# Two-layer cross-attention on one core: image scores copied by VectorE, and the second pair's two norm products side by side

## The chip, the core and the metric

The kernel runs on one core of a Trainium2 chip. A core has a matrix engine (TensorE, called PE in the profile, with its weight loads shown apart as PEld), VectorE (DVE), ScalarE (ACT), GpSimd (POOL) and SyncE (SP, which here only issues transfers). Each engine works through its own queue in order; they wait for each other by semaphores. Matmuls write to PSUM, a small memory of eight banks per partition; VectorE and ScalarE read their results from there. The metric is the device time of one execution in microseconds.

## The reference

Two cross-attention layers with image prompts follow each other, on 16 batches of 256 query positions and 320 channels, 20 heads of 16. The context has 256 rows of 512 features. The first layer takes 77 rows as text and the other 179 as image tokens; the second takes 252 as text and the last 4 as image tokens. The part that matters here is the second layer, cut to its core:

```python
q, k_t, v_t = heads(hidden @ W_q), heads(text @ W_k), heads(text @ W_v)
probs_t = softmax(q @ k_t.T * 0.25)
text_out = probs_t @ v_t
attn = q @ heads(ip @ W_k_ip).T * 0.25            # 4 image scores per query and head
qsem = l2norm(probs_t @ text)                     # per head, 512 features
sem = qsem @ l2norm(ip).T
probs_ip = softmax(attn + 0.5 * sem) * spatial_mask
out = (text_out + probs_ip @ v_ip) @ W_out + b_out + hidden
```

The length of `probs_t @ text` is needed for `l2norm`. The kernel gets its square as p^T G p, where G = text text^T is one matrix for each batch: it multiplies G with the probabilities, multiplies the product element by element with the probabilities, and sums over the text rows. These are the "norm products" below.

## The kernel before, in words

Work goes in *slots*: one slot is one batch and one group of four heads, so there are 5 slots for a batch, 80 (`NS`) for the first layer and 80 for the second, one after the other. What PE does, and in which order, is written out by hand in `slot0` and `slot1`: a slot yields functions, which are run at that place, and numbers such as 0.33, 0.67 and 1.0. At a number, `fill(k + number)` runs all tasks that are due by then (projections, keys, values, closing of a batch), each with a table of due times. So a number in `slot1` is a place for other work. On PE this program order is also the order on the chip. For VectorE, ScalarE, POOL and SP the order is planned when the kernel is built, from dependencies and estimated times; `queued` adds an order-only edge that puts an instruction behind the last `anchor` of its engine.

In the second layer, slot k does the following on PE.

- `attend1(k - 2)` (lines 855 to 864) makes the weighted values of the slot two before: sixteen matmul records in line 861, and then the *zone* matmuls of line 863 with their eight records. These add the column sums of `W[k, u][:, 0]`, the finished squared lengths, for the two head pairs u = 0 and 1. They need the sums of line 853.
- `both1(k, 0)` and, later, `both1(k, 1)` (lines 773 to 800) do the transposed scores of slot k (tile T, line 787), and the plain scores of slot k + 2 (tile S, line 792, two banks and one buffer). VectorE takes the maxima over the text columns of S (line 793), ScalarE the exponentials of T (line 798) into P, and `image_scores` copies the four image columns of each head out of S (line 810, 128 x 16 elements).
- `norm1(k - 1, u, n)` (lines 843 to 853) is a norm product for pair u, half n: four matmuls of 512 columns for n = 0, three for n = 1 (line 848), into a bank of the tag X. VectorE multiplies the result with W (line 851); for u = 1 and n = 1 it writes the result back to the PSUM bank, and VectorE then adds it to the first half in line 853. For u = 0 POOL does that addition.
- `rounded1(k, u)` (lines 834 to 839) prepares the next slot's products: ScalarE rounds half of P (line 838, tile ctb), POOL takes the difference to P (line 839, tile wt). The rounded halves go to two buffers in turn, so the rounding of pair u waits until the previous slot's products of that pair have read theirs.
- `maxima(k + 2)` (lines 822 to 832) turns the maxima by two small matmuls (line 826), ScalarE copies them (line 828) and issues two transfers that write them to the query rows.
- `stacks(k + LEAD)` loads the rows of queries and keys for a later slot by SP.

The other matmuls of that layer come from fills: line 212 (keys, values and G of the next batch), line 519 (projections of queries and outputs; their results are read out by lines 527 and 528, or 766), line 969 (closing of a batch, read by lines 970, 747, 749 and 751). All of these and the norm products use the tag X, with three buffers.

Of the kernel before, what the change touches and what calls it, by code (L numbers as in the profile page):

```python
# [10 lines left out]
AF = mybir.ActivationFunctionType  # L11
# [17 lines left out]
SCALE = 0.25  # L29
# [8 lines left out]
NS = B * NG  # L38
# [10 lines left out]
def xattn2(  # L49
# [27 lines left out]
    nc = tc.nc  # L77
# [11 lines left out]
    def bank(tag="X"):  # L89
        return ps.tile([128, 512], F32, tag=tag, name=tag, bufs=BANKS[tag])  # L90

    def scores():

        return ps.tile([128, 1024], F32, tag="S", name="S", bufs=1).rearrange("p (h t) -> p h t", h=4)
# [4 lines left out]
    def buf(tag, shape, dtype=F32, bufs=1, name=None):  # L99
        if tag in ("wB", "wD", "vr", "raw"):  # L100
            return sb.tile(shape, dtype, tag=tag, name=name or tag, bufs=bufs)
        size = 1
        for d in shape[1:]:
            size *= d
        if tag not in slots:
            slots[tag] = [0, dtype] + [const_tile([128, max(size, words.get(tag, 0))], f"{tag}_{i}", dtype) for i in range(bufs)]
        n, kind, *ring = slots[tag]
        assert kind == dtype and len(ring) == bufs, tag
        slots[tag][0] += 1
        t = ring[n % bufs][: shape[0], :size]  # L110
        names = "abcd"[: len(shape) - 1]
        if len(names) > 1:
            t = t.rearrange(f"p ({' '.join(names)}) -> p {' '.join(names)}", **dict(zip(names, shape[1:])))
        return t
# [17 lines left out]
    def queued(inst, *behind):  # L132

        for other in behind or [anchors.get(inst.ins.engine)]:
            if other is not None:
                tc.add_manual_dep(
                    inst.ins, other.ins.name, mybir.DependencyInfo(mybir.DependencyClass.NoSync, mybir.DependencyReason.DATA), reason="order"
                )
        return inst

    def anchor(inst):
        anchors[inst.ins.engine] = inst
        return inst
# [459 lines left out]
    QK, P, W, R = {}, {}, {}, {}  # L603
# [76 lines left out]
    def attend0(k):  # L680
        b, g = divmod(k, NG)
        v, pv = get("v0", b), bank("P")
        for vt in range(3):
            values0(k, pv, v, vt)
        settle0(b, g, pv)
# [87 lines left out]
    def both1(k, t):  # L773

        a = k + 2 < 2 * NS and QK[k + 2] 
        c = NS <= k < 2 * NS and QK[k]
        if a:
            if t == 0:
                maxes[k + 2] = buf("mn", [128, 4, 4], FR, bufs=2)[:, :2]
            sp = scores()  # L780
        if c:
            st = [bank("T").rearrange("p (h t) -> p h t", h=2) for u in range(2)]
            lo = (0, DUP)[t]
            for j in range(2):
                for u in range(2):
                    rows = slice(64 * u, 64 * u + KS1)
                    mm(st[u][:, j], c[1][rows, j, lo : lo + 128], c[0][rows, j], start=True, stop=True)  # L787
        if a:
            for j in range(2):
                for u in range(2):  # L790
                    rows = slice(64 * u, 64 * u + XROW)
                    mm(sp[:, 2 * u + j], a[0][rows, j, t * 128 : (t + 1) * 128], a[1][rows, j], start=True, stop=True)  # L792
            anchor(nc.vector.tensor_reduce(maxes[k + 2][:, t], sp[:, :, :T1], axis=AX.X, op=ALU.max))  # L793
        if c:
            for u in range(2):
                if t == 0:
                    P[k, u] = buf("P", [128, 2, 2, S], bufs=SIZES["NP"])
                anchor(queued(nc.scalar.activation(P[k, u][:, t], st[u], AF.Exp, scale=SCALE)))  # L798
        if a:
            image_scores(k + 2 - NS, t, sp)  # L800

    sims = {}

    def image_scores(n, t, sp):
        b, g = divmod(n, NG)
        if (g, t) == (0, 0):
            sims[b] = buf("sr", [128, 2, 4, NG, NIP], bufs=2)
        sr = sims[b]
        src = sp.rearrange("p (u j) t -> p u j t", u=2)[:, :, :, T1:]
        anchor(nc.scalar.copy(sr[:, t, :, g].rearrange("p (j u) n -> p u j n", u=2), src))  # L810
        if (g, t) == (NG - 1, 1):
            later(0.3, lambda: image_scores_out(b))

    def image_scores_out(b):
        sid = dram.tile([S, 4, NG * NIP], F32, tag="sid", name="sid", bufs=2)
        dma(sid.rearrange("(t p) s c -> p t (s c)", p=128), sims[b].rearrange("p t s g n -> p t (s g n)"))
        si = results["si", b] = buf("si", [128, 8, NG * NIP], bufs=2)
        parts = sid.rearrange("(f r) s c -> r s f c", r=32)
        for s in range(4):
            later(1.3, lambda s=s: dma(si[32 * s : 32 * s + 32], parts[:, s]))  # L820
# [13 lines left out]
    def rounded1(k, u):  # L834
        R[k, u] = buf("ctb", [128, 2, 2, S], FR, bufs=SIZES["CTB"], name="ph")
        W[k, u] = buf("wB", [128, 2, 2, S], bufs=SIZES["WB"], name="wt")
        for t in range(2):
            nc.scalar.activation(R[k, u][:, t], P[k, u][:, t], AF.Copy, scale=0.5)  # L838
            anchor(nc.gpsimd.tensor_sub(W[k, u][:, t], P[k, u][:, t], f(R[k, u][:, t])))  # L839
# [3 lines left out]
    def norm1(k, u, n):  # L843

        gm = get("t1", k // NG - B)[1]
        yp = bank().rearrange("p (h t) -> p h t", h=2)
        for i, (gb, kt) in enumerate(blocks[n]):
            mm(yp, gm[:, gb], R[k, u][:, kt], start=i == 0, stop=i == len(blocks[n]) - 1)  # L848
        w = W[k, u]
        product = yp if n and u else w[:, n]  # L850
        nc.vector.tensor_mul(product, yp, w[:, n])  # L851
        if n:
            (nc.vector if u else nc.gpsimd).tensor_add(w[:, 0], w[:, 0], product)  # L853

    def attend1(k):
        b, g = divmod(k - NS, NG)
        v, pv = get("t1", b)[0], bank("P")
        for n in range(2):
            for s in range(4):
                h = V1W * (4 * g + s)  # L860
                mm(pv[32 * s : 32 * s + 32, :S], v[:, n, h : h + 32], P[k, s % 2][:, n, s // 2], start=n == 0, stop=False)  # L861
        for s in range(4):
            mm(pv[32 * s : 32 * s + 32, :S], zone, W[k, s % 2][:, 0, s // 2], start=False, stop=True)  # L863
        settle1(b, g, pv)

    def slot1(k):
        last = k - 1 if NS < k <= 2 * NS else None
        mine = k < 2 * NS
        if k == NS:
            yield lambda: maxima(k + 1)  # L870
        elif k == NS + 1:
            yield lambda: attend0(k - 2)
        else:
            yield lambda: attend1(k - 2)
        yield lambda: both1(k, 0)
        if last:
            yield lambda: norm1(last, 0, 0)
        yield 0.33
        if last:
            yield lambda: norm1(last, 0, 1)  # L880
        yield lambda: both1(k, 1)
        if mine:
            yield lambda: rounded1(k, 0)
        yield lambda: stacks(k + LEAD)
        if last:
            yield lambda: norm1(last, 1, 0)
        yield 0.67
        if last:
            yield lambda: norm1(last, 1, 1)
        if mine:  # L890
            yield lambda: rounded1(k, 1)
        yield lambda: maxima(k + 2)
        yield 1.0

# [124 lines left out]
    def later(slots, make):  # L1019
        delayed.append((clock[0] + slots, make))  # L1020
# [26 lines left out]
    for c in range(B // 2):  # L1047
        n, k = 10 * c, [("k0", c)] if c else []
# [11 lines left out]
    for b in range(B):  # L1060
        n = NS + 5 * b
# [17 lines left out]
    def stacks(k, parts="KQ"):  # L1079
        if 0 <= k < NS:  # L1080
            stacks0(k, parts)
        elif k < 2 * NS and "K" in parts:
            stacks1(k)

    def ahead(k, t):
        if k < NS:
            score0(k, t)
        else:
            both1(k - 2, t)

    def maxima(k):
        if k < 2 * NS:
            (maxima0 if k < NS else maxima1)(k)
# [43 lines left out]
    with tc.manual_schedule(engines=PINNED):  # L1137
        for k in range(2 * NS + 2):
            clock[0] = k
            for part in (slot0 if k < NS else slot1)(k):  # L1140
                if callable(part):
                    part()
                else:
                    fill(k + part)
        fill(999)
# [81 lines left out]
```

## Time and profile before

| | us |
|---|---|
| median of 3 runs | 1545.48 (1541.51 to 1552.83) |
| the profiled execution | 1544.94 |
| its span, first to last instruction | 1542.8 |
| PE busy | 1475.5 (96%) |
| VectorE busy | 1166.4 (76%) |
| ScalarE busy | 967.6 (63%) |
| POOL busy | 1146.1 (74%) |

The mean granted clock of PE is 0.987 of full speed. Busy means that at least one instruction of the engine was under way. Matmuls are pipelined and their ends are modelled, so PE's share overstates how well it is used: a wait of some tenths of a microsecond can lie inside a "busy" stretch. Start times of groups tell more than their lengths. A row of the timeline gives start, length, engine, line, operation, tiles and count; a bracket gives the idle time before it and what ended it. A row of the waits gives the waiting engine, tile and line, what it waited for, total us, times, and the longest. A row of groups ends with busy us, mean ns of one, and the idle time before.

### The profile page before, as it was taken

How to read it: one execution, taken by the hardware profiler on the slowest of the kernel's cores; microseconds unless marked ns; L12 is line 12 of the kernel's file. 1: busy time of each engine (PE TensorE's matmuls, PEld its weight loads, DVE VectorE, ACT ScalarE, POOL GpSimd, SP SyncE). 2: the span in 40 equal slices, each digit the busy share in tenths (PEclk: the TensorE clock that was granted, in tenths of full speed). 3: DMA queues.
4: the chain of work that ended last, by engine and by line, in shares of the span. 5: the costliest groups of instructions: out<-in, count | busy, mean ns of one | idle time of the engine just before them, and what ended most of it. 6: DMA issues, size and time to landing. Idle time of an engine off the chain costs nothing.

```text
span 1542.8 us, 35099 instructions
## 1 busy us (share of the span) xinstructions
PE 1475.5 (96%) x12522; PEld 1186.1 (77%) x12522; DVE 1166.4 (76%) x2424; ACT 967.6 (63%) x2233; POOL 1146.1 (74%) x1161
## 2 busy tenths in 40 slices
PE   7899999999999998899999999999999999999997
PEld 6778888888888886677777777777777777777765
DVE  5567676767677778777888778778877887888796
ACT  5567676767676866656556556655565556566563
POOL 3259797979797867886777777777787787777685
PEclk9899999999999999999999999999999999999999
DMA  7656665657565665464534443434344434433311
GB/s 218 168 166 174 168 174 161 185 149 193 149 184 150 183 172 148 117 193 133 155 98 115 130 142 94 137 112 150 90 140 124 137 99 133 134 98 112 109 30 59
DMA packets 226986, 215.38 MB, mean 140 GB/s; under 512 B 49722, under 2 KB 210716, under 8 KB 226812
## 3 DMA queue, kind: packets, MB, share of 16 engines
q1 hardware_dynamic: 225072, 211.84, 47.9%
q8 instruction: 99, 1.62, 0.5%
q10 hardware_dynamic: 1740, 1.30, 0.3%
q14 instruction: 75, 0.61, 0.1%
HBM read 122.17 MB, written 89.49 MB: 137 GB/s over the span
## 4 chain that ended last, share of the span: by engine, by line
PE 84%; DVE 7%; DMA 3%; issue 2%; POOL 1%; ACT 1%; SPq 0%; DVEq 0%; POOLq 0%; ACTq 0%
PE X L212 22%; PE X L848 18%; PE X L519 11%; PE P L710 7%; PE S L649 5%; PE T L787 4%; PE T L672 4%; PE P L861 4%; PE P L863 3%; PE S L792 3%; PE X L969 1%; PE X L568 1%; DVE X L851 1%; DVE wt L853 1%; POOL P L678 1%
## 5 line engine op out<-in xcount | busy, mean ns | idle before, releaser
L678 POOL TENSOR_TENSOR P<-P,rs 128x512 f32<-128x512 f32 x320 | 411.9, 1309 | 157.7 <-ACT P L675 157.5
L839 POOL TENSOR_TENSOR wt<-P,ctb 128x512 f32<-128x512 f32 x320 | 413.3, 1304 | 113.0 <-ACT ctb L838 108.0
L848 PE MATMUL X<-ctb,gm 128*128 128x512 f32 x1120 | 330.1, 412 | 0.8 <-DVE wt L851 0.8
L675 ACT ACTIVATE P<-T 128x512 f32<-128x512 f32 x320 | 174.9, 593 | 105.5 <-PE T L672 95.8
L798 ACT ACTIVATE P<-T 128x512 f32<-128x512 f32 x320 | 174.1, 598 | 91.2 <-PE T L787 81.6
L848 PEld LDWEIGHTS X<-ctb,gm 128*128 128x128 f32 x1120 | 189.4, 188 | 46.6 <-DVE wt L851 1.2
L838 ACT ACTIVATE ctb<-P 128x512 fp32r<-128x512 f32 x320 | 195.4, 632 | 42.5 <-PE X L848 42.3
L793 DVE TENSOR_REDUCE mn<-S 128x4 fp32r<-128x1008 f32 x160 | 191.9, 1200 | 0.5 <-PE S L792 0.5
L851 DVE TENSOR_TENSOR wt<-X,wt 128x512 f32<-128x512 f32 x240 | 163.6, 682 | 24.8 <-PE X L848 23.9
L651 DVE TENSOR_REDUCE mn<-S 128x4 fp32r<-128x716 f32 x160 | 142.4, 890 | 0.0
L710 PE MATMUL P<-P,vr 128*32 128x256 f32 x1920 | 125.0, 391 | 4.4 <-DVE mx L574 2.6
L649 PE MATMUL S<-ks,qs 125*128 125x256 f32 x640 | 116.7, 306 | 0.9 <-DVE mn L651 0.9
L649 PEld LDWEIGHTS S<-ks,qs 125*128 125x128 f32 x640 | 88.0, 193 | 34.2 <-issue 32.1
L519 PE MATMUL X<-hq,wE 128*128 128x256 f32 x768 | 109.3, 286 | 4.4 <-ACT hq L508 3.6
L519 PE MATMUL X<-ho,wF 128*128 128x256 f32 x768 | 109.0, 284 | 2.3 <-DVE ho L751 2.0
L519 PEld LDWEIGHTS X<-hq,wE 128*128 128x128 f32 x768 | 102.1, 193 | 8.1 <-ACT hq L508 4.0
L672 PE MATMUL T<-qs,ks 127*128 127x256 f32 x640 | 105.5, 288 | 1.9 <-DVE kst L148 1.9
L212 PE MATMUL X<-cta,wA 128*128 128x252 f32 (+1 forms) x720 | 100.1, 285 | 6.3 <-ACT wA L147 6.3
L853 POOL TENSOR_TENSOR wt<-wt 128x512 f32<-128x512 f32 x80 | 103.8, 1298 | 2.5 <-DVE wt L851 1.4
L519 PEld LDWEIGHTS X<-ho,wF 128*128 128x128 f32 x768 | 100.5, 190 | 6.7 <-DVE ho L751 2.7
L212 PEld LDWEIGHTS X<-cta,wA 128*128 128x128 f32 x720 | 93.1, 193 | 9.0 <-ACT wA L147 6.5
L721 DVE STREAM_TRANSPOSE nt<-P 128x512 f32<-128x512 f32 x80 | 57.0, 713 | 50.6 <-PE P L710 50.6
(199 smaller groups left out, 2948.5 us busy)
## 6 DMA issues: line engine op xcount, KB each, us to landing
qd<-q SPq DMA_DIRECT2D x96, 384.0 KB
kd<-kst SPq DMA_DIRECT2D x73, 256.0 KB
rawc<-in_cT_dram SPq DMA_DIRECT2D x60, 256.0 KB
qs<-qd SPq DMA_DIRECT2D x80, 192.0 KB
ks<-kd SPq DMA_DIRECT2D x80, 192.0 KB
ks<-kd SPq DMA_DIRECT2D x160, 96.0 KB
qs<-qd SPq DMA_DIRECT2D x160, 96.0 KB
kd<-kst SPq DMA_DIRECT2D x21, 512.0 KB
```

The lines of the kernel that those rows point to most:

```text
L212: last = mm(out, lhs(a, k), rhs(b, k), start=i == 0, stop=i == len(terms) - 1)
L519: mm(pp, w(s, k, slice(m * 128, (m + 1) * 128)), a[:, t], start=i == 0, stop=i == len(terms) - 1)
L649: mm(sp[:, h], Q[: XROW + T0, h, t * 128 : (t + 1) * 128], K[: XROW + T0, h], start=True, stop=True)
L675: exp = anchor(nc.scalar.activation(pt, st[p], AF.Exp, scale=SCALE))
L678: anchor(nc.gpsimd.tensor_mul(pt, pt, rs[:, t : t + 1].to_broadcast([128, 2, S])))
L710: mm(pv[32 * s : 32 * s + 32, o : o + S], v[:, vt, h : h + 32], P[k, s // 2][:, t, s % 2], start=vt < 2, stop=vt != 1,)
L793: anchor(nc.vector.tensor_reduce(maxes[k + 2][:, t], sp[:, :, :T1], axis=AX.X, op=ALU.max))
L798: anchor(queued(nc.scalar.activation(P[k, u][:, t], st[u], AF.Exp, scale=SCALE)))
L838: nc.scalar.activation(R[k, u][:, t], P[k, u][:, t], AF.Copy, scale=0.5)
L839: anchor(nc.gpsimd.tensor_sub(W[k, u][:, t], P[k, u][:, t], f(R[k, u][:, t])))
L848: mm(yp, gm[:, gb], R[k, u][:, kt], start=i == 0, stop=i == len(blocks[n]) - 1)
L851: nc.vector.tensor_mul(product, yp, w[:, n])
```

## The change

Two things are changed.

First, the copy of the image scores moves from ScalarE to VectorE. It is issued directly behind the maximum that reads the same score tile, is ordered behind it by `queued`, and becomes VectorE's new anchor. The exponentials become plain anchors of ScalarE: they are no longer ordered behind the last anchor there, which was the previous copy.

Second, the order inside `slot1`: the second pair's second product, `norm1(last, 1, 1)`, comes directly behind its first, `norm1(last, 1, 0)`, and `rounded1(k, 1)` behind it. The 0.67 fill, which stood between the two products, now comes after all of these. `maxima(k + 2)` stays behind the fill.

```diff
             anchor(nc.vector.tensor_reduce(maxes[k + 2][:, t], sp[:, :, :T1], axis=AX.X, op=ALU.max))
+            image_scores(k + 2 - NS, t, sp)
         if c:
             for u in range(2):
                 if t == 0:
                     P[k, u] = buf("P", [128, 2, 2, S], bufs=SIZES["NP"])
-                anchor(queued(nc.scalar.activation(P[k, u][:, t], st[u], AF.Exp, scale=SCALE)))
-        if a:
-            image_scores(k + 2 - NS, t, sp)
+                anchor(nc.scalar.activation(P[k, u][:, t], st[u], AF.Exp, scale=SCALE))
...
-        anchor(nc.scalar.copy(sr[:, t, :, g].rearrange("p (j u) n -> p u j n", u=2), src))
+        anchor(queued(nc.vector.tensor_copy(sr[:, t, :, g].rearrange("p (j u) n -> p u j n", u=2), src)))
...
         yield lambda: stacks(k + LEAD)
         if last:
             yield lambda: norm1(last, 1, 0)
-        yield 0.67
-        if last:
             yield lambda: norm1(last, 1, 1)
         if mine:
             yield lambda: rounded1(k, 1)
+        yield 0.67
         yield lambda: maxima(k + 2)
         yield 1.0
```

## The prediction

> **What bounds the kernel now.** The page comes first: the matrix engine (PE) is said to be busy 96% of the span, VectorE (DVE) 76%, ScalarE (ACT) 63%, GpSimd (POOL) 74%. Only the second layer runs the changed lines, so the next view is the table of stretches (PE, its weight loads, DVE, ACT, POOL, each with its busy time), cut where that layer's pattern repeats: 52.8 us for one batch of five slots. The first row below is the page's, the second the table's.
>
> ```profile
> PE 1475.5 (96%) x12522; PEld 1186.1 (77%) x12522; DVE 1166.4 (76%) x2424; ACT 967.6 (63%) x2233; POOL 1146.1 (74%) x1161
> ...
> 1086.80:1139.60 52.80, 52.02 (x420) 39.62 (x419) 42.31 (x81) 31.62 (x79) 39.53 (x44) 1.00 0.42 123
> ```
>
> PE 52.02 of 52.80 us looks like an engine with nothing left to win. It is not, since the ends of pipelined matmuls are modelled and a short wait is counted as busy. So I read the waits between 770 and 1500 us (total, times, longest), and then PE's own timeline.
>
> ```profile
> PE P L863 <- DVE wt L853: 10.3, 14, 0.8
> ...
> PEld P L863 <- DVE wt L853: 28.7, 44, 1.3
> ...
> ACT sr L810 <- DVE mn L793: 70.2, 81, 2.0
> ```
>
> One wait dominates on PE: the zone matmuls of line 863, for the last VectorE add of line 853. 730 us hold 13.8 batches, and 44 waits are 3.2 in each: about three slots of five. The third row is ScalarE idling until a maximum is done so that it can copy the image scores; ScalarE is the least busy engine and PE does not wait for it, so this row is worth nothing by itself. The same batch on PE (start, length, engine, line, tile, count), cut to the slots that I call A, B, C, D and E in order of time (A's zones begin at 1090.57, B's at 1101.30, C's at 1113.37, D's at 1122.25):
>
> ```profile
> 1086.33 1.19 PE L848 MATMUL X<-ctb,gm 128*128 128x512 f32 x4
> ...
> 1088.77 0.86 PE L848 MATMUL X<-ctb,gm 128*128 128x512 f32 x3
> ...
> 1090.57 0.59 PE L863 MATMUL P<-wt,zone 128*32 128x256 f32 x2
> 1091.91 0.63 PE L863 MATMUL P<-wt,zone 128*32 128x256 f32 x6 [0.75 <-DVE wt L853]
> 1092.47 0.51 PE L787 MATMUL T<-qs,ks 50*128 50x256 f32 x4
> ...
> 1097.55 1.20 PE L848 MATMUL X<-ctb,gm 128*128 128x512 f32 x4
> 1098.59 0.59 PE L969 MATMUL X<-rs,rs 128*128 128x256 f32 x2
> 1098.83 1.05 PE L848 MATMUL X<-ctb,gm 128*128 128x512 f32 x3
> 1099.71 0.28 PE L826 MATMUL X<-ident_r,mn 128*4 128x128 f32 x2
> 1099.84 0.64 PE L969 MATMUL X<-rs,rs 128*128 128x256 f32 x2
> ...
> 1101.30 0.97 PE L863 MATMUL P<-wt,zone 128*32 128x256 f32 x8
> 1102.20 0.51 PE L787 MATMUL T<-qs,ks 50*128 50x256 f32 x4
> ...
> 1110.00 1.16 PE L519 MATMUL X<-ho,wF 128*128 128x256 f32 x8
> ...
> 1113.37 0.61 PE L863 MATMUL P<-wt,zone 128*32 128x256 f32 x8
> 1113.91 0.50 PE L787 MATMUL T<-qs,ks 50*128 50x256 f32 x4
> ...
> 1118.47 1.19 PE L848 MATMUL X<-ctb,gm 128*128 128x512 f32 x4
> ...
> 1122.25 1.26 PE L863 MATMUL P<-wt,zone 128*32 128x256 f32 x8
> 1123.44 0.51 PE L787 MATMUL T<-qs,ks 50*128 50x256 f32 x4
> ...
> 1131.16 1.95 PE L212 MATMUL X<-wC,cta 128*128 128x320 f32 x12
> ```
>
> Eight zone matmuls that wait for nothing take 0.61 us (1113.37, slot C); by the start of the next group, some 0.54. Slot A needs 1092.47 - 1090.57 = 1.90, slot B 0.90, slot D 1.19. The excess is 1.36 + 0.36 + 0.65 = **2.37 us per batch**, 4.5% of it, three times the 0.78 that the busy column admits. This is the layer's removable time; the rest of PE stands back to back.
>
> **The change, part by part: the adjacent products.** PE does the same matmuls; only the second pair's second product (line 848 x3) trades places with the work of the 0.67 fill. So PE reaches the zones at the same instant as before, and what moves is the moment at which VectorE can start the second product. VectorE in slots A, B and D:
>
> ```profile
> 1086.58 1.20 DVE L793 TENSOR_REDUCE mn<-S 128x4 fp32r<-128x1008 f32 x1
> 1087.69 0.68 DVE L851 TENSOR_TENSOR wt<-X,wt 128x512 f32<-128x512 f32 x1
> ...
> 1091.18 0.67 DVE L853 TENSOR_TENSOR wt<-wt,X 128x512 f32<-128x512 f32 x1
> 1092.60 0.45 DVE L907 STREAM_TRANSPOSE nt<-P 128x256 f32<-128x256 f32 x1 [0.74 <-PE P L863]
> ...
> 1096.69 0.42 DVE L528 TENSOR_TENSOR q<-X,q 128x256 fp32r<-128x256 f32 x1 [0.88 <-ACT q L527]
> ...
> 1097.66 1.21 DVE L793 TENSOR_REDUCE mn<-S 128x4 fp32r<-128x1008 f32 x1
> ...
> 1100.94 0.65 DVE L853 TENSOR_TENSOR wt<-wt,X 128x512 f32<-128x512 f32 x1
> 1101.51 0.41 DVE L749 TENSOR_TENSOR ho<-X,ho 128x256 fp32r<-128x256 f32 x1
> ...
> 1118.58 1.21 DVE L793 TENSOR_REDUCE mn<-S 128x4 fp32r<-128x1008 f32 x1
> 1119.77 0.69 DVE L851 TENSOR_TENSOR wt<-X,wt 128x512 f32<-128x512 f32 x1
> ...
> 1122.14 0.69 DVE L853 TENSOR_TENSOR wt<-wt,X 128x512 f32<-128x512 f32 x1
> ```
>
> In slot A the add ends at 1091.18 + 0.67 = 1091.85, 1.28 after the zones began; in B at 1101.59; in D at 1122.83. After the change the chain is: maximum, image copy (0.2, priced below), multiply 0.69, multiply 0.69, add 0.69. The second product leaves PE at the latest 1.04 + 0.88 = 1.92 after the pair began (slot B's rows: 1097.55 to 1098.59, 1098.83 to 1099.71), which is never the last to come:
> - A: copy from 1087.69, multiplies from 1087.89 and 1088.58, add 1089.27 to 1089.96. Product there at 1088.25. The zones need it at about 1090.7 (two of eight run before): 0.7 to spare.
> - B: maximum to 1098.87, add done at 1101.14; needed at about 1101.45: 0.3 to spare.
> - D: copy from 1119.77, add done at 1122.04; needed at about 1122.4: 0.35 to spare.
>
> So all three waits go, 2.37 us per batch, if VectorE does the pair in one run. The sum must also let VectorE follow a faster PE. From slot A to slot B it has 0.74 and 0.88 idle (the bracketed waits above), 1.62 in all; A's 1.36 and the copies of two slots, 4 x 0.2, ask for 2.16. The missing half microsecond may be paid by PE in some batches; I book 0.27, half of it, and take **2.1 us per batch**.
>
> **The image copies.** 160 copies leave ScalarE and come to VectorE, right behind the maximum that reads the same tile. The trace shows no such copy on VectorE. The nearest rows:
>
> ```profile
> L810 ACT COPY sr<-S 128x16 f32<-128x16 f32 x160 | 27.5, 172 | 75.0 <-DVE mn L793 74.9
> ...
> L910 DVE RECIPROCAL P<-nt 128x8 f32<-128x8 f32 x80 | 16.7, 209 | 2.5
> ...
> L571 DVE TENSOR_TENSOR sp<-sp,X 128x77 f32<-128x77 f32 x32 | 7.2, 228 | 7.5 <-ACT sp L570 7.1
> ```
>
> Nothing at all is the lower end (a wait taken from ScalarE could pay for it), 228 ns for 77 columns from the same kind of memory the upper; I take 0.2, by the eight-column row. Ten per batch are 2.0 us: VectorE goes from 42.3 to 44.3 of a batch that shrinks to 50.7, 87%. Inside the three chains the 0.2 is already counted. In C and E it lies under PE work. Were the cover gone everywhere, PE would pay 2.0 a batch and nearly nothing would be won. The copy also frees the score tile; behind the maximum on one engine that is no later than by a second engine.
>
> The Trainium skill (Perfetto Trace Analysis, "Optimizing Scalar/DVE Operations") speaks against this part: where VectorE is saturated, work should go to ScalarE, and it gives about 125 ns of access overhead for VectorE on PSUM against 51 for ScalarE. From that an estimate of some 0.14 us a copy, 1.4 a batch. The 87% above says that VectorE is near that state, not in it.
>
> **ScalarE and POOL.** ScalarE loses 74.9 us of waiting in line, and its exponentials no longer stand behind the copy; PE waited for neither, so I book nothing. The second pair's rounding is issued before the fill instead of behind it: ScalarE can start when the second product is off PE, about one fill sooner (0.24 us in slot B, from 1098.59 to 1098.83), and POOL's subtractions follow. POOL at 39.5 of 52.8 has room; nothing booked. No DMA moves past another: stacks and the maxima's two writes keep their places on SP's and ScalarE's queues.
>
> **The sum.** The zones run through the whole of the layer, by the line's own summary (shortest, middle and longest in ns, first and last start):
>
> ```profile
> L863 PE MATMUL P<-wt,zone x640: 379/379/404, 710.0 to 1526.0; 128*32 128x256 f32 x160
> ```
>
> 816 us at 52.8 are 15.5 batches, the reference's 16 with a shorter end: 16 x 2.1 = 34 us. The first and last batch differ but have such waits too. The profiled execution took 1544.94 (span 1542.8), half a microsecond under the median 1545.48: 1545 - 34 = **1511 us**, 2.2% less. If all of 2.37 goes, 1507; if VectorE cannot follow and gives back 0.8 to 1.0 a batch, 1525.
>
> **Rivals.** *The queue order takes it back.* VectorE's order is planned at build time, and before, an evacuation stood between the two multiplies. If the fill's evacuation, which waits for ScalarE (0.88 in the row of L528), still runs ahead of the pair's second multiply, the add comes no sooner, and the copy's 0.2 comes on top of three waits: +0.6 a batch, +10 us, **1555**; with a 0.88 wait newly in front in one slot, +1.5, 1569. For it: the planner does not know the real durations. Against: the second product now leaves PE before the fill even starts.
>
> *Banks.* This is the slower one. The adjacent second product keeps its bank through multiply and add. If the three X banks went strictly round, the maxima would take the first product's bank and the next group the second's. In B the second L969 group, now at 1099.84, would start when the add ends, 1101.14: +1.3, less the 0.36 won. C and E also have a group behind the maxima (1110.00, 1131.16); priced as B, +1.3 each. 0.94 + 2.6 - 1.36 - 0.65 = +1.5 a batch, +24 us: **1569**. It decides where a group other than the zones follows the maxima within 1.3 us. Against it stands slot B itself, with one row more of ScalarE:
>
> ```profile
> 1100.57 0.34 ACT L828 CAST mt<-X 4x256 fp32r<-4x256 f32 x1
> ```
>
> At 1100.6 four X tiles are alive: the first L969 group (begun 1098.59, last read by L749 at 1101.51), the product of 1098.83 (read until L853's end, 1101.59), the maxima (read at 1100.57) and the second L969 group (begun 1099.84). Three banks in rotation could not hold them, so a longer-held product need not block the next group. The skill's same page ("Optimization Strategy") says that a repeating gap can mean too little PSUM; by this trace PE's repeating gap is a data wait, not a bank.
>
> **How the numbers follow.** The forecast with its own range 1503 to 1530, full or shortened by VectorE: 0.58. Queue order: 0.22 near 1545 to 1558, 0.12 above that; banks: 0.08. The range 1502 to 1560 takes the forecast and the milder order case and leaves out the slower ones and the tails. About 1% is what a measurement of this kernel can tell from no change (runs from 1541.51 to 1552.83). Faster by over 1%: 0.58; within: 0.22; slower: 0.20.
>
> **What would show it.** Right: a batch of about 50.7 us in the second layer; the waits of L863 for L853 near zero; on VectorE maximum, copy, multiply, multiply, add in one run; the copy near 0.2 us; ScalarE's 74.9 us wait gone; the first layer unchanged at its lines. Wrong: L863 still over 0.61 us in slots A and D with an evacuation between the multiplies (order); an idle PE before the group behind the maxima, released by L853 (banks); PE's score matmuls of line 792 waiting for the copy, or VectorE without idle time all batch long (VectorE is the bound). New idle of PE before 700 us would mean that the plan of the other queues shifted, which I cannot see from here.

## The result: no change

Over twelve runs each, the changed kernel takes 1548.72 us in the median (1544.69 to 1551.72) and the kernel before 1548.34 (1541.51 to 1552.83). The ratio is 1.0004, with a 95% interval of 0.9988 to 1.0019: no difference within 0.2%, where 2.2% less was forecast. The profiled execution took 1551.27 us (span 1549.5). It lies a little above its median, that of before a little below, so the two traces stand 6 us further apart than the two kernels. Of all executions reported below one, of the experiment that loads the image values early, took 3121.82 us, twice the usual time; its ratio is taken without it.

Lines have moved up by one or two: the products are now line 847, VectorE's multiplies 850 and their add 852, the values 860, the zones 862, the maxima's matmul 825 with ScalarE's copy of it 827, the closing rows 967. The slots keep their letters; A's zones begin at 1095.11 in the batch shown.

### The profile page after: what moved, and what is told of

The parts are those of the page before. It is cut to its first block, busy times and chain, and to the rows that moved or that the text cites. A ratio compares the mean times of both kernels' runs of the same rounds, so it can differ in the third digit from the quotient of the medians.

```text
span 1549.5 us, 35139 instructions
## 1 busy us (share of the span) xinstructions
PE 1469.5 (95%) x12522; PEld 1191.1 (77%) x12522; DVE 1183.0 (76%) x2584; ACT 957.5 (62%) x2073; POOL 1143.0 (74%) x1161
## 5 line engine op out<-in xcount | busy, mean ns | idle before, releaser
L847 PE MATMUL X<-ctb,gm 128*128 128x512 f32 x1120 | 316.2, 411 | 0.6 <-DVE kst L148 0.6
L847 PEld LDWEIGHTS X<-ctb,gm 128*128 128x128 f32 x1120 | 193.6, 188 | 52.0 <-DVE kst L148 1.1
L837 ACT ACTIVATE ctb<-P 128x512 fp32r<-128x512 f32 x320 | 190.4, 632 | 36.9 <-PE X L847 33.9
```

## The profile after, beside the one before

First the page's row of engines, then the row that sums up the zones (its last two times are the first and the last start), then the groups of the moved copy and of VectorE's line 510 over the whole run (busy us, mean ns, idle before).

```profile
PE 1469.5 (95%) x12522; PEld 1191.1 (77%) x12522; DVE 1183.0 (76%) x2584; ACT 957.5 (62%) x2073; POOL 1143.0 (74%) x1161
```

```profile
L862 PE MATMUL P<-wt,zone x640: 379/379/404, 710.5 to 1530.7; 128*32 128x256 f32 x160
```

```profile
L510 DVE SCALAR_TENSOR_TENSOR hq<-hq,tmask,xq 128x256 fp32r<-128x256 f32 x32 | 29.6, 926 | 0.2 <-ACT hq L508 0.2
L809 DVE COPY sr<-S 128x16 f32<-128x16 f32 x160 | 26.2, 164 | 0.0
```

The first layer is as it was: the zones begin at 710.5 us, half a microsecond from before. They now run for 820.2 us, where they took 816.0. The copy is as small as forecast, 0.164 us. So the 2.1 us a batch did not come in the layer in which they were booked. The waits between 770 and 1500 us (total, times, longest) say what PE stands for instead:

```profile
DVE rs L960 <- DMA rs<-vipd: 14.9, 13, 2.1
...
PE X L967 <- ACT mt L827: 11.4, 13, 0.9
...
PE P L862 <- DVE wt L852: 6.1, 13, 0.5
...
PE X L825 <- DVE mn L793: 4.7, 11, 1.1
```

The zones' wait stood 44 times in its weight-load row before, three slots of five; now it stands 13 times, one slot. But two waits of PE are new, also about once a batch (before, the first did not occur and the second once, for 0.4 us): a closing row behind ScalarE's copy of the maxima, and the maxima's matmul behind a maximum. PE's timeline of one batch has all three:

```profile
1095.11 0.59 PE L862 MATMUL P<-wt,zone 128*32 128x256 f32 x2
1096.18 0.63 PE L862 MATMUL P<-wt,zone 128*32 128x256 f32 x6 [0.47 <-DVE wt L852]
1096.74 0.50 PE L787 MATMUL T<-qs,ks 50*128 50x256 f32 x4
...
1103.57 0.59 PE L967 MATMUL X<-rs,rs 128*128 128x256 f32 x2
1103.81 0.47 PE L825 MATMUL X<-ident_r,mn 128*4 128x128 f32 x2
1105.14 0.70 PE L967 MATMUL X<-rs,rs 128*128 128x256 f32 x2 [0.87 <-ACT mt L827]
...
1106.66 0.61 PE L862 MATMUL P<-wt,zone 128*32 128x256 f32 x8
1107.21 0.50 PE L787 MATMUL T<-qs,ks 50*128 50x256 f32 x4
...
1114.85 0.22 PE L825 MATMUL X<-ident_r,mn 128*4 128x128 f32 x1
1116.19 0.22 PE L825 MATMUL X<-ident_r,mn 128*4 128x128 f32 x1 [1.11 <-DVE mn L793]
...
1128.65 0.61 PE L862 MATMUL P<-wt,zone 128*32 128x256 f32 x8
1129.19 0.50 PE L787 MATMUL T<-qs,ks 50*128 50x256 f32 x4
```

By starts, as in the prediction: slot A's zones take 1.63, 1.09 over the undisturbed 0.54 (1.36 before); B takes 0.55 and D 0.54, nothing over. Won: 0.27 + 0.36 + 0.65 = 1.28. Lost in B: the second closing row starts 1.33 behind the maxima's matmul, where it was 0.13 (1099.71 to 1099.84): 1.20. Lost in C: the two maxima matmuls start 1.34 apart instead of together, over a microsecond in this batch; over the batches the loss there is mostly 0.6, and 1.0 and 1.4 in two. A typical batch is 53.2 us long against 52.8.

VectorE in slots A and C, and ScalarE in slot B, show who is late:

```profile
1092.62 0.68 DVE L850 TENSOR_TENSOR wt<-X,wt 128x512 f32<-128x512 f32 x1
1093.22 1.50 DVE L510 SCALAR_TENSOR_TENSOR hq<-hq,tmask,xq 128x256 fp32r<-128x256 f32 x1
1094.64 0.69 DVE L850 TENSOR_TENSOR X<-X,wt 128x512 f32<-128x512 f32 x1
1095.24 0.29 DVE L491 SCALAR_TENSOR_TENSOR v1t<-X,tmask,rn 128x80 f32<-128x80 f32 x1
1095.45 0.67 DVE L852 TENSOR_TENSOR wt<-wt,X 128x512 f32<-128x512 f32 x1
...
1113.86 0.56 DVE L960 TENSOR_TENSOR rs<-rs,nt 128x384 f32<-128x384 f32 x1 [2.11 <-DMA rs<-vipd]
1114.34 0.68 DVE L850 TENSOR_TENSOR wt<-X,wt 128x512 f32<-128x512 f32 x1
1114.93 1.20 DVE L793 TENSOR_REDUCE mn<-S 128x4 fp32r<-128x1008 f32 x1
```

```profile
1103.17 1.68 ACT L837 ACTIVATE ctb<-P 128x512 fp32r<-128x512 f32 x3
1104.75 0.34 ACT L827 CAST mt<-X 4x256 fp32r<-4x256 f32 x1
```

- **Slot A.** The pair is not done in one run. The plan puts line 510, a step of splitting the next batch's input, between the two multiplies, and it takes 1.50 us there.
- **Slot B.** ScalarE copies the maxima out of their bank only behind three roundings, at 1104.75. The second closing row starts 0.39 later, just past the end of that copy.
- **Slot C.** VectorE stands 2.11 us in front of a product whose operand comes by DMA (line 960, the image values times their mask). The multiply and the maximum behind it in the queue are late by as much, and the maxima's matmul waits for that maximum. In the kernel before, the same product did not wait, as VectorE's timeline there shows:

```profile
1107.30 0.56 DVE L962 TENSOR_TENSOR rs<-rs,nt 128x384 f32<-128x384 f32 x1
```

  Two things moved here. Counted from the issue of that transfer, VectorE is ready for the product mostly 2.15 us behind it in the change, where it was 2.8 before. And the transfer lands later: the product starts 2.6 to 4.3 us behind the issue, where it started at 2.7 to 3.2 in all but one batch before, mostly without a wait. In most batches of the change, the load ahead of it on SP's queue is issued only 0.47 us earlier, where it was 2.18 before. Whether this is why it lands later was not tried.

## The experiments

Theory A: the new order wins 1.30 us a batch at the zones and loses some 1.8 to the waits of slots B and C, which arise from where the build's plan puts other work once the order is changed; taken away, the forecast gain appears. Theory B: it is the copies, which fill VectorE until it cannot follow.

All numbers in one table. In its names, "late image product" or "late product" is the edit of slot C below, "maxima first" one of slot B, and "both edits" these two. The kernel before ran beside each, at 1545.3 to 1548.3 us, so the ratios are the thing to compare. The layer is the distance from the first to the last zones in the summary row of the profiled run; the batch is the typical distance from one slot A to the next on PE's timeline; the ratio is to the kernel before.

| kernel | median us | ratio, 95% interval | layer | batch |
|---|---|---|---|---|
| before | 1548.34 | | 816.0 | 52.8 |
| the change | 1548.72 | 1.0004, 0.9988 to 1.0019 | 820.2 | 53.2 |
| copy alone | 1556.18 | 1.0078, 1.0055 to 1.0101 | 827.6 | 54.0 |
| order alone | 1537.34 | 0.9962, 0.9941 to 0.9983 | 805.7 | 52.1 |
| image values loaded early | 1547.99 | 1.0015, 0.9999 to 1.003 | 819.4 | 53.2 |
| closing row earlier | 1545.12 | 1.0003, 0.9987 to 1.002 | 818.6 | 52.9 |
| change, late image product | 1531.5 | 0.9921, 0.9897 to 0.9946 | 802.0 | 52.3 |
| change, maxima first | 1540.72 | 0.9966, 0.9952 to 0.998 | 812.5 | 52.7 |
| order, both edits | 1527.43 | 0.9886, 0.9865 to 0.9907 | 797.6 | 52.0 |
| change, both edits and anchored add | 1525.07 | 0.9869, 0.9848 to 0.9889 | 797.5 | 52.0 |
| the same, closing row later | 1524.68 | 0.9866, 0.9842 to 0.989 | 794.5 | 51.7 |
| change, late product, anchored add | 1528.01 | 0.9889, 0.9867 to 0.9911 | 797.4 | 51.9 |
| before, late product | 1539.96 | 0.997, 0.9956 to 0.9984 | 811.3 | 52.8 |
| order, late product | 1521.16 | 0.9839, 0.9816 to 0.9862 | 789.0 | 51.2 |
| the same, closing row later | 1515.95 | 0.9816, 0.98 to 0.9832 | 786.3 | 50.8 |
| order, late product, spare copies | 1542.24 | 0.998, 0.9967 to 0.9993 | 812.6 | 53.0 |
| change, late product, exponentials as before | 1531.85 | 0.9915, 0.9896 to 0.9935 | 801.9 | 52.3 |
| spare copies, line 510 behind the add | 1531.1 | 0.9897, 0.9879 to 0.9914 | 802.0 | 52.2 |
| change, late product, line 510 behind the add | 1526.45 | 0.9865, 0.9844 to 0.9885 | 797.8 | 51.9 |
| the same, closing row later | 1518.93 | 0.9818, 0.9797 to 0.984 | 788.3 | 51.2 |

### The two halves of the change

Each half was run by itself: the copy with the old order in `slot1`, and the new order with ScalarE's copy.

> Only the copy of the image scores moves to VectorE; the order of the slot stays as before. Theory A (the new order wins 1.30 us a batch at the zones and loses 1.8 to two waits it creates, for the maxima's bank and for a transfer): the zones keep their 2.4 us of waiting a batch, no wait appears behind the maxima, and the time is that of before within 0.5%, 1544 to 1556 us. Theory B (the copies fill VectorE and eat what the new order wins, some 20 us): this kernel has the cost without the gain, 1562 us or more.

> Only the order of the slot changes; ScalarE keeps the copy. Theory A: the zones wait about 1.1 us a batch instead of 2.4, the maxima and the group behind them about 1.8, as in the changed kernel: 1542 to 1554 us. Theory B: without copies on VectorE the whole gain stands, 1515 to 1525 us.

The order is worth 0.4%, the copy costs 0.8%; 0.9962 times 1.0078 is 1.0040, within 0.4% of the result. The halves have these rows in their waits, the copy alone first:

```profile
PE X L968 <- ACT mt L827: 11.6, 12, 1.0
PE P L862 <- DVE wt L852: 8.7, 14, 0.7
```

```profile
DVE rs L961 <- DMA rs<-vipd: 11.2, 12, 2.3
PE X L826 <- DVE mn L793: 8.0, 12, 0.9
PE P L861 <- ACT mt L828: 7.7, 12, 0.6
```

With the order alone the zones' wait is all but gone: its weight-load row stands 4 times instead of 44, and by starts the zones of slots A, B and D take 0.54 to 0.55 us in nearly every batch. There the prediction's main step does what it said. But slot C's wait is there without any copy, and so is a wait behind ScalarE's copy of the maxima, one group further on. With the copy alone slot B's wait is there too. So the two waits belong to neither half alone. Neither half came out at a time that one of the theories gave. The copy alone lies at the very top of theory A's range and 6 us under theory B's; the order alone lies 5 us under theory A's, which had left 1.1 us of waiting at the zones, and 12 over theory B's.

### Slot C: a product that waits for a transfer

```diff
-        nc.vector.transpose(pT, pi.rearrange("p f c -> p (f c)"))
-        nc.vector.tensor_mul(vb, vb, w1["bmask"])
+        turn = nc.vector.transpose(pT, pi.rearrange("p f c -> p (f c)"))
+        queued(nc.vector.tensor_mul(vb, vb, w1["bmask"]), turn)
```

The first try moved the load (its `dma` call goes to the first step of `image_softmax`), the second moved the product behind a transpose that comes much later; its result isn't needed before.

> The changed kernel, but the transfer of the image values (the operand of VectorE's multiplication in line 960) is issued at the first step of the image softmax instead of the last. Theory A: VectorE no longer stands 2.1 us for that transfer, so the maxima of slot C lose their wait of 0.6 us (1.4 in some batches), some 0.7 x 15 = 10 us: 1535 to 1541 us. If that wait only moved on to the next instruction or VectorE is simply full (theory B): 1546 to 1551, with the wait for the maximum still there.

> The changed kernel, but VectorE's multiplication of line 960 is ordered behind the transpose of the same step, some 25 us later than it now stands in VectorE's queue, when its transfer has long landed (the earlier issue of that transfer had moved nothing). Theory A: the wait of the maxima's matmul for the maximum in slot C (0.6 us a batch, 1.0 to 1.4 in some) goes: 13 x 0.7 = 9 us, 1535 to 1543 us. Theory B (VectorE is simply too full, the stand of 2.1 us only replaces other waiting): that wait stays and the time is 1545 to 1551.

The early load moved nothing: VectorE's wait for it is 13.8 us instead of 14.9, and the transfer is still issued right behind the same other load. I put that down to its buffer, which comes free only with the closing rows of the batch before; that was not tried. The late product took the wait of slot C away, from the list and from the timeline, and the time is 0.8% under before, where the change is level with it. As a control, the same edit in the kernel before, whose product does not wait:

> Control: the kernel before, with nothing but the multiplication of line 962 ordered late. In the kernel before VectorE waited for that transfer 0.4 us in the whole of the stretch from 770 to 1500 us, so theory A (the new order made that wait) gives no gain here: 1542 to 1552 us, ratio 0.998 to 1.003. If the edit is good by itself, whatever the order: 1535 or less.

0.3% less, just under theory A's range, with a steady batch as long as it was. So at most 0.3 of the 0.8% is something that any version would have gained; the rest is a wait that the change had made.

### Slot B: the bank behind the maxima

Two edits: the second closing row's due time goes from 9 to 8.67, so that it stands elsewhere; and the maxima are issued ahead of `rounded1(k, 1)`, whose roundings are queued behind ScalarE's copy of the maxima.

```diff
-        task(("c1", b), shifted(..., 8.67, 9, 9.33, 10, 11.67, 13.33), ...)
+        task(("c1", b), shifted(..., 8.67, 8.67, 9.33, 10, 11.67, 13.33), ...)
```

```diff
-        nc.scalar.copy(mt[:, 0], mp[:4, :S])
+        turned[0] = nc.scalar.copy(mt[:, 0], mp[:4, :S])
...
-            nc.scalar.activation(R[k, u][:, t], P[k, u][:, t], AF.Copy, scale=0.5)
+            half = nc.scalar.activation(R[k, u][:, t], P[k, u][:, t], AF.Copy, scale=0.5)
+            if u and turned[0] is not None:
+                queued(half, turned[0])
...
-        if mine:
-            yield lambda: rounded1(k, 1)
         yield 0.67
         yield lambda: maxima(k + 2)
+        if mine:
+            yield lambda: rounded1(k, 1)
```

> The changed kernel, but the second row of a batch's closing (two matmuls of line 967) is due in the 0.67 fill, ahead of the maxima, instead of behind them. Theory A: it no longer waits for ScalarE's copy of the maxima behind three roundings, 1.22 us a batch: 1548 - 1.1 x 15 = 1528 to 1535 us. If the bank wait only passes to the maxima or to the zones: 1544 to 1552.

> The changed kernel, but ScalarE copies the maxima ahead of the second pair's two roundings, so that the bank of the maxima is read out about 1.1 us sooner. Theory A (the group behind the maxima takes their bank, and that bank waits for ScalarE's queue): the wait of line 967's second group in slot B falls from 1.22 us to 0.2 or less, 13 x 1.1 = 14 us: 1530 to 1538. Rival: the wait is for another bank, such as the product's, and stays: 1545 to 1551.

Moving the row did not remove the wait, it handed it to the values (line 860), released now by VectorE's add, which holds the bank of the product:

```profile
PE P L860 <- DVE wt L852: 10.5, 13, 1.1
```

The values write tile P and the product lies in tile X, which suggests that a bank does not stay with one tag, although the kernel's text gives X three buffers. In that trace the add ends at 1096.78 and the values start at 1096.84. This is read from the wait; no run tests it.

With the maxima first, ScalarE's copy of them comes earlier and the wait of the closing row shrinks from 11.4 to 5.4 us, 1.23 to 0.81 a batch by starts:

```profile
PE X L971 <- ACT mt L829: 5.4, 12, 0.5
```

So the wait is released by that copy, as theory A has it, but it is not gone, and the time lies between the two ranges that were expected. I read this as PE being short of banks just there: who is blocked depends on who comes next.

### Both edits together

> The new order with the copy left on ScalarE, and both of the edits above. Its batch of 52.08 us holds 0.7 + 0.2 (slot B, behind the maxima) and 0.9 (slot C, maxima); the zones wait for nothing. Theory A: 50.4 us a batch, 1537 - 24 = 1510 to 1518 us. If only one of the two goes: 1522 to 1530. If the waits pass on to other places: 1534 to 1540.

> The changed kernel (copy on VectorE) with both edits, and with the addition of line 852 made an anchor of VectorE, so that the split of line 510 (1.50 us between the pair's two multiplications in slot A) is ordered behind it. Theory A: zones 0 instead of 1.10, slot B 0, slot C 0: 53.18 - 2.9 = 50.3 us a batch, 1548 - 38 = 1508 to 1518 us, level with the order alone, since the copy itself costs VectorE under 0.1 us from start to start. Theory B (copies fill VectorE): 8 us or more above the run with the copy on ScalarE.

> The last kernel (copy on VectorE, new order, all three edits: 52.05 us a batch with 0.81 + 0.39 in slot B behind the maxima, 0.47 at slot A's zones and 0.5 ahead of a product), but the second row of a batch's closing is made in slot C together with the third, so that in slot B no group but the values follows the maxima. Theory A (in slot B the banks are used up, and whatever follows the maxima waits for a bank): the values now take that place, they wait as in the run with the row ahead of the maxima (1.1 us) or, with one bank less in use, not at all: 51.3 us a batch and 1525 - 11 = 1511 to 1519 us. If the wait stays whatever follows: 1522 to 1528.

> The changed kernel with the multiplication of line 960 late and the addition of line 852 as an anchor, the roundings where the change put them. With the late multiplication alone a batch took 52.32 us, of which 1.36 at the zones of slot A behind line 510. Theory A: those 1.36 go, except what the split then delays (0.5 ahead of a product, as in the run with all edits): 51.5 us a batch, 1531 - 12 = 1515 to 1523 us. Rival: the split, later, holds up the next projection by as much: 1529 to 1533.

> The new order with the copy left on ScalarE and the multiplication late, the roundings where the change put them. From 52.08 us a batch the 0.9 of slot C goes: 51.2 us, 1537 - 12 = 1522 to 1528 us by theory A. Against the run with the same edit and the copy on VectorE (1531) it tells what the copy is worth once the transfer is out of the way: equal within 4 us by theory A, 8 us or more less by theory B (the copies fill VectorE).

The anchored add makes line 852 an anchor of VectorE, so that line 510 is queued behind it; the later closing row has the second due time at 9.33 instead of 9. All five beat both kernels, by 1.1 to 1.6%. But theory A's times were missed: the first four are 5 to 9 us slower than it gave. By starts the zones of slot A still wait 0.85 us a batch in the first, where lines 491 and 510 stand between the second multiply and the add, and about 0.5 in the next three. The plainest, the new order with the late product alone, is the best of them: 1521.16 us. In it next to nothing is left at the zones (7 waits of 44), and the maxima-first edit, which helped the change, makes it 6 us slower. But with VectorE's copy in the place of ScalarE's, the same kernel takes 1531.5, where theory A had expected the two within 4 us of each other and theory B 8 us or more apart. Theory A does not say why.

### Is it the copies' time, or where the plan puts line 510?

First the copies were added to the best order without taking anything from ScalarE, into a tile that nobody reads; then the copy was moved with the exponentials queued as before.

```diff
             anchor(nc.vector.tensor_reduce(maxes[k + 2][:, t], sp[:, :, :T1], axis=AX.X, op=ALU.max))
+            spare = buf("spare", [128, 4, NIP], bufs=2)
+            anchor(queued(nc.vector.tensor_copy(spare, sp[:, :, T1:])))
```

> The new order with the late product and ScalarE's copy kept (1521.16 us), and beside it the change's copy on VectorE behind each maximum, into a spare tile that nobody reads: the copies are added to VectorE and nothing is taken from ScalarE. Theory B (the copies' time on VectorE, or the extra instruction's place in its order, is what holds the copied kernels 7 to 10 us up): about 1530, batch 52.0 or more, slot A's zones waiting about 1.1. Theory A (VectorE takes 0.08 us a copy from start to start and has room): 1521 within 3, batch 51.2, and the 10 us of the copied kernel come from the plan that the loosened exponentials and the moved anchor give.

> The change with the late product (1531.5 us, batch 52.32, slot A's zones waiting 1.36 because the 1.50 us product of line 510 stands between the pair's two multiplies), but the exponentials left free in the plan as a queued instruction, as the change has them, against the form that keeps them fixed as an anchor alone. If the loosened exponentials put line 510 there, the time goes to about 1521 and the multiplies stand together; if the copy on VectorE itself does, it stays at 1531 within 3 and line 510 stays between the multiplies.

(The second expectation has the two forms the wrong way round: it is the change that leaves the exponentials as plain anchors, and this kernel that queues them.) The exponentials have nothing to do with it: 1531.85 against 1531.5. The spare copies cost 21 us, 1.9 a batch, more than twice what theory B gave them. Theory B seems right, until VectorE's queue is read in slot A, first without and then with the copies:

```profile
1076.01 1.19 DVE L793 TENSOR_REDUCE mn<-S 128x4 fp32r<-128x1008 f32 x1
1077.12 0.67 DVE L851 TENSOR_TENSOR wt<-X,wt 128x512 f32<-128x512 f32 x1
1077.72 0.69 DVE L851 TENSOR_TENSOR X<-X,wt 128x512 f32<-128x512 f32 x1
1078.44 0.69 DVE L853 TENSOR_TENSOR wt<-wt,X 128x512 f32<-128x512 f32 x1
1079.05 1.58 DVE L510 SCALAR_TENSOR_TENSOR hq<-hq,tmask,xq 128x256 fp32r<-128x256 f32 x1
```

```profile
1086.58 1.20 DVE L793 TENSOR_REDUCE mn<-S 128x4 fp32r<-128x1008 f32 x1
1087.69 0.16 DVE L795 COPY spare<-S 128x16 f32<-128x16 f32 x1
1087.78 0.67 DVE L853 TENSOR_TENSOR wt<-X,wt 128x512 f32<-128x512 f32 x1
1088.37 0.68 DVE L853 TENSOR_TENSOR X<-X,wt 128x512 f32<-128x512 f32 x1
...
1089.18 1.39 DVE L510 SCALAR_TENSOR_TENSOR hq<-hq,tmask,xq 128x256 fp32r<-128x256 f32 x1
1090.50 0.67 DVE L855 TENSOR_TENSOR wt<-wt,X 128x512 f32<-128x512 f32 x1
```

The copy holds the next multiply up by 0.09 us (1087.69 to 1087.78). Line 510, which stood behind the add, now stands in front of it and holds it up by 1.32. Its place alone was then changed, by queueing it behind the pair's add: with the spare copies, in the change, and in the change with the closing row at 9.33. The best order had got that later row too.

```diff
+        sink = order(nc.vector.scalar_tensor_tensor(hl[:, 2], f(hl[:, 2]), neg, src[:, 2], op0=ALU.mult, op1=ALU.add))
+        if 1 in summed:
+            queued(sink, summed[1])
...
+            summed[u] = (nc.vector if u else nc.gpsimd).tensor_add(w[:, 0], w[:, 0], product)
```

> The new order with the late product (1521.16 us, batch 51.15), and the closing rows moved in the plan from 8.67, 9 and 9.33 to 8.67, 9.33 and 9.33. What is left of PE's waiting there is 1.04 us a batch at the values behind slot B's second closing row (0.33 of it is there in the kernel before too), put down to ScalarE's copy of the maxima. Theory A (the wait passes to the group that follows the maxima, whichever it is): with both closing rows together that group is another, some 0.7 of the 1.04 goes, batch about 50.5, time about 1511. If the bank is short whatever follows, the wait only changes its name: batch 51.1 within 0.2, time 1518 to 1524.

> The new order with the late product and the spare copies on VectorE (1542.24 us, batch 53.0, slot A's zones waiting 1.78), where the 1.39 us product of line 510 stands on VectorE between the pair's second multiply and its add; here it is queued behind that add. If the place of that product is the price of the copies: the zones' wait falls to 0.5 or less, batch 51.7, time 1520 to 1526. If it is VectorE's time for the copies: the wait and the time stay, 1538 to 1545.

> The change with the late product (1531.5 us, batch 52.32, slot A's zones waiting 1.36 with line 510 between the two multiplies), and the product of line 510 queued behind the pair's add. Place of the product: wait 0.5 or less, batch 51.4 to 51.5, time 1517 to 1521, as good as the new order with ScalarE's copy (1521.2). Time for the copies: 1529 to 1534, as before the edit.

> As the run before it, with the closing rows moved to 8.67, 9.33 and 9.33, which took 5.2 us (51.15 to 50.80 a batch) from the new order with ScalarE's copy. Slot B's values wait 0.8 a batch there; half of it goes: 5 us under the run before it, 1512 to 1516, as good as the best kernel so far (1515.95). If VectorE has no room left for the copies, the wait turns up at the zones instead and the two are within 2 us of each other.

Line 510's place is worth 11 us of the spare copies' 21 and 5 of the change's 10. By starts slot A's zones then wait some 0.46 us a batch, where they waited 1.78 and 1.36. The bank in slot B takes much of the gain back: the waits of the change with line 510 behind the add are

```profile
PE X L971 <- ACT mt L831: 11.4, 13, 0.9
...
PEld P L866 <- DVE wt L856: 7.5, 17, 0.9
```

so both times expected of line 510's place alone were missed by 5 us: slot B's bank wait, by starts at the closing row and the values behind it, was 0.9 and 0.65 us a batch in the kernels without the edit and came to 1.47 and 1.22. The later closing row removes that as well: 5.2 us in the new order (half of what theory A expected; the zones then wait 0.42 in slot B), and 7.5 in the change, 3 us short of what was expected. At the end the two stand at 1515.95 and 1518.93, with intervals that overlap. With everything else in place, then, VectorE's 160 copies cost at most a few microseconds. **Most of what the copies cost, they cost through the plan:** of the 10 us between 1531.5 and 1521.16, 3 are left. The zones of slot A still wait 0.46 us a batch in the change, and none in the new order, which is about the 0.4 by which its batch is longer. VectorE has line 491 between the second multiply and the add there, and the late image product, 0.85 us long, right ahead of the maximum; which of these it is was not tried. Why the build's planner moves line 510 when a copy joins that queue was not tried.

The best kernel found is the new order, with ScalarE's copy, the late image product and the later closing row: 0.9816 of before. The change itself, with the three placings, comes to 0.9818. Only the late product was also put into the kernel before. What the other two placings would give that kernel, with its old order, is open, so a part of the 1.8% may not need the change.

## Why the prediction was wrong

- **The removable time** was right. Slots A, B and D wait 2.37 us a batch; the order alone all but empties the zones' row, and the best kernel's batch is 50.8 us against the forecast 50.7, its layer 29.7 us shorter against 34, though with two placings that the forecast did not have.
- **"So all three waits go, 2.37 us per batch, if VectorE does the pair in one run": this step failed**, in slot A. The rows that were quoted jump from 1087.69 to 1091.18. Between them the trace of before had

```profile
1089.18 0.96 DVE L510 SCALAR_TENSOR_TENSOR hq<-hq,tmask,xq 128x256 fp32r<-128x256 f32 x1
1090.07 0.68 DVE L851 TENSOR_TENSOR X<-X,wt 128x512 f32<-128x512 f32 x1
```

  that is, line 510 already stood between the multiplies, in a place where it cost less, as the second product was complete only at 1089.63 (1088.77 + 0.86): it held the second multiply up by 0.44. Lines 494 and 498 stood between that multiply and the add, another 0.51 (1090.67 to 1091.18). Line 510 stays there in the change, and 1.09 of 1.36 stays with it. The rival "queue order" had the mechanism and named the wrong instruction, the fill's evacuation.
- **"The rest of PE stands back to back"** and, of ScalarE, POOL and transfers, **"nothing booked"**: this failed by as much again. Slots B and C lost some 1.2 and 0.6 to 1.4 a batch to an instruction that was on no path before: a copy behind three roundings, and a product that waits for a transfer. For the former the prediction saw the roundings move ahead of the maxima and booked nothing for what stands behind them on ScalarE. For the latter it said that no DMA moves past another, which is so; but VectorE comes to the product 0.65 us earlier and the transfer lands later.
- **The banks rival** was argued away because four X tiles were alive at 1100.6. Slot B nevertheless loses what the rival priced there, 1.2 to 1.3, with another releaser: the maxima's bank, not the product's, which came only where the closing row was moved. In C and E, where it was priced as well, there is no bank wait.
- **The copy's price** was right, 0.2 forecast and 0.164 long, 0.08 to 0.09 from start to start. What was booked for it outside the three chains, nothing, was not, since an instruction costs also what the plan does with its neighbours: the copy alone made a batch 1.2 us longer and the kernel 0.8% slower, and the spare copies cost 1.9 a batch. That is near the 2.0 which the prediction gave for copies without any cover, but most of it by line 510's place. The Trainium skill's caution (Perfetto Trace Analysis, "Optimizing Scalar/DVE Operations") against loading VectorE points the right way, but not for its reason: VectorE was busy 76% of the span before and after.
- Of the signs, ScalarE's wait for the maximum and the first layer came out as said, the batch of 50.7 us and the one run on VectorE did not.

## What to carry to other kernels

Where an order is planned at build time, a change that makes one wait vanish should be given the explicit edges that hold its gain: which instruction may not stand inside the chain, and which that waits for a transfer may not stand ahead of it. Read every row between the first and the last link of the chain, those of other work too, before writing that the chain will run without a break. And test halves with each new wait taken away: the sum of two halves was close to zero here, while the same change with three placings is 1.8% faster.

## What the runs showed of the hardware

Line 510 takes 0.54 us or 1.58, with the same operands. What decides is GpSimd. The order alone has the short case:

```profile
1089.19 0.54 DVE L510 SCALAR_TENSOR_TENSOR hq<-hq,tmask,xq 128x256 fp32r<-128x256 f32 x1
```

GpSimd's instruction under way when line 510 starts, in four kernels: the change (line 510 from 1093.22 to 1094.72), the kernel before (1089.18 to 1090.14), the order with the late product (1079.05 to 1080.63) and the order alone (1089.19 to 1089.73):

```profile
1093.14 1.29 POOL L838 TENSOR_TENSOR wt<-P,ctb 128x512 f32<-128x512 f32 x1
```

```profile
1088.58 1.29 POOL L839 TENSOR_TENSOR wt<-P,ctb 128x512 f32<-128x512 f32 x1
```

```profile
1079.04 1.30 POOL L839 TENSOR_TENSOR wt<-P,ctb 128x512 f32<-128x512 f32 x1
```

```profile
1088.14 1.31 POOL L839 TENSOR_TENSOR wt<-P,ctb 128x512 f32<-128x512 f32 x1
```

They end at 1094.43, 1089.87, 1080.34 and 1089.45. Line 510 ends 0.27 to 0.29 later in all four: it stands until POOL's instruction is done and then runs. The product of line 960 behaves in the same way (0.56 with POOL idle, 1.46 where POOL's instruction had 1.05 left). The multiplies of line 850, which read one operand from PSUM, take 0.65 to 0.70 in all 320 cases of the change. The Trainium skill (SBUF — State Buffer, "Who interferes with whom") says so: a VectorE instruction with two inputs in SBUF and a GpSimd instruction that reads SBUF exclude each other, and the second to issue blocks until the first has finished. The traces agree. For a forecast this means that such a row has no price of its own: line 510's 0.96 in the trace of before was what POOL had left at that moment, and 1.50 was due wherever it moved to the start of POOL's next.
